# The start of a graph layer: where the first rows' numbers come from, and the order of the work up to the first pass

## The chip, the cores and the metric

The kernel runs on one core of one Trainium2 chip. The metric is the time of one execution in microseconds (us), the median of several runs. The core has five engines that each work through their own list of instructions in order and wait for each other by semaphores: TensorE (PE in the profile; its weight loads are PEld), VectorE (DVE), ScalarE (ACT), GpSimd (POOL) and SyncE (SP), which only issues transfers here. 16 DMA engines carry the transfers of SP's queue and of GpSimd's.

## The reference

A graph has 12500 nodes of 128 features and 200000 edges, sorted by destination. Each row of x is normalised and clipped at zero (h). Each edge has a score from its two nodes and a decay by its weight; of every node's incoming edges the 16 best are kept, a softmax over them weighs the messages, and the node's output is x plus a clipped sum.

```
h = max(layernorm(x), 0)
score = einsum("md,md->m", (h @ W_Q.T)[dst], (h @ W_K.T)[src]) / sqrt(128) * exp(-edge_weight)
keep the 16 best scores of each dst; alpha = softmax over the kept
agg = segment_sum(alpha * (h[src] @ W_msg.T), dst)
out = x + relu(h @ W_self.T + agg)
```

## The kernel before

**Tiling.** The edges stand in 112 groups of 14 chunks of 128 edges (G, GC). For each chunk GpSimd issues one indirect transfer (L177, called a gather here) which fetches the 128 rows that the chunk's edges name as their sources: 64 KB into hs[:, j, :]. A group's buffer hs is one of eight. 1548 gathers are issued, one after the other. The built program lets each gather wait for the landing of the eighth gather before it.

**Two kinds of gathers.** The rows of h are first written to a table in DRAM, h_tab. It is not ready at the start, so the first four groups (RAW, 56 gathers) fetch raw rows of x, which are normalised in the buffer afterwards: statistics by row_stats (L202), then one ScalarE activation for a row of 128 edges (normed, L223), or two VectorE instructions (L249, L251). From group 4 on a group is let go in pairs of gathers (let_go, L191): VectorE copies two columns of indices into a tile ix (L199), and the two gathers read it. This copy stands in VectorE's list at a chosen place, so a gather can't start before VectorE has come that far.

**Before the loop (L270 to L476).** The order is written by hand. SP loads src as rows (L290 to L294), then x in six parts (L313), then the weights, the destinations and the edge weights. GpSimd makes constants and clears alz[1] (L337). VectorE turns the sources into float (L361, L362), TensorE transposes them so that each chunk's 128 numbers stand in 128 partitions (to_columns, L296), VectorE converts them to indices (L364), and the raw gathers follow. The six parts of x are then normalised by VectorE and ScalarE in turn and written to h_tab (L373). After that come the raw statistics of groups 0 and 1 (L387), the distances of the destinations (rel, L416), the raw rows of group 0 (L418), a comparison of neighbours (L420) and a scan over it (L422), which gives every edge its place among its node's edges, the raw rows of group 1 (L424), and three sets of 14 or 15 transposes or products through PSUM: pd from rel (L432, L434), pd from the scan (L437), the decays exp(-weight) (L439). They all go through the PSUM banks "q", of which there are three. VectorE ends with checks (L441 to L470) and the last nodes' numbers, idxo (L476).

**Pools.** These tiles lie in the pools edges and prep. Both are given back at the end of this part, and the pool win of the main loop gets their space.

**The loop (L762).** Pass i, from -3 on, works on several groups at once: for group i the scores (L618), for group i+1 the distances (far_of, L571; away, L594, each a matmul into the one bank "a" and a ScalarE square), for i-1 the places of the scores, for i-2 the choice of the 16 best, for i-3 the weighted sums (L709), which are the last reader of that group's hs, for i-4 and i-5 the output. Before the first scores, group 0 needs hT (L552), q, far, to_e (L576), pdT (L585), aw and opo (L598). The raw rows of groups 2 and 3 get their statistics at the end of pass 0 (L836) and are normalised in passes 1 and 2, three times three rows on ScalarE and four on VectorE (raw_finished, L243). From pass 2 on pass i lets go of the last pairs of group i+4 and the first two of group i+5 (more, L775):

```
            g, k = (i + 4, k + 2) if k < 5 else (i + 5, k - 5)
```

So the first pair of group 8, whose hs is the buffer that held group 0, is let go in pass 3, at more(5), after the sums of group 0.

Of the kernel before, what the change touches and what calls it, by code (L numbers as in the profile page):

```python
# [76 lines left out]
def gnn_layer(  # L77
# [55 lines left out]
    def bank(tag, bufs):  # L133
        return psum.tile([P, 512], F32, tag=tag, bufs=bufs, name=tag)
# [36 lines left out]
    T = [{} for _ in range(G)]  # L171

    def gather(g, j0, j1, index, table=h_tab):
        if j0 == 0:
            T[g]["hs"] = rows_pool.tile([P, GC, D], F32, name="hs", bufs=8)
        for j in range(j0, j1):
            nc.gpsimd.indirect_dma_start(  # L177
                out=T[g]["hs"][:, j, :], out_offset=None, in_=table[0:N, :],
                in_offset=bass.IndirectOffsetOnAxis(ap=index(j), axis=0))
# [43 lines left out]
    def normed(rows, n0, n1, rs, sm):  # L223

        if n0 == 0:
            nc.vector.reciprocal(rs, rs)
            nc.vector.scalar_tensor_tensor(sm, sm, -0.5, rs, op0=OP.mult, op1=OP.mult)
        for t in range(n0, n1):
            nc.scalar.activation(rows[:, t, :], rows[:, t, :], AF.Relu, bias=sm[:, t:t + 1],
                                 scale=rs[:, t:t + 1])  # L230
# [3 lines left out]
        T[g]["raw"] = row_stats(rows_pool, T[g]["hs"], own[g], f"r{g % 2}")  # L234

    def raw_normed(g):
        normed(T[g]["hs"], 0, own[g], *T[g]["raw"])


    def raw_begun(g):  # L240
        normed(T[g]["hs"], 0, 1, *T[g]["raw"])

    def raw_finished(g, part):  # L243
        rows, (rs, sm) = T[g]["hs"], T[g]["raw"]
        if part < 3:
            normed(rows, 1 + 3 * part, 4 + 3 * part, rs, sm)
            return
        for t in range(10, own[g]):
            nc.vector.tensor_scalar(rows[:, t, :], rows[:, t, :], rs[:, t:t + 1], sm[:, t:t + 1],  # L249
                                    op0=OP.mult, op1=OP.add)  # L250
            nc.vector.tensor_scalar(rows[:, t, :], rows[:, t, :], 0.0, None, op0=OP.max)  # L251

    w0 = rows_pool.tile([P, NJ], F32, name="w0")
    zpad = rows_pool.tile([P, D], F32, name="zpad")
# [12 lines left out]
    sizes = [n for n in sizes + [left] if n]  # L267
    cuts = [(a, b) for a, b in ((0, HP - HP % 16), (HP - HP % 16, HP)) if a < b]
    by_part = lambda a: a[0:N, :].rearrange("(p t) d -> p t d", t=HT)
    with tc.tile_pool(name="edges", bufs=1) as ep, ExitStack() as stage:  # L270
        prep = stage.enter_context(tc.tile_pool(name="prep", bufs=1))
        RL = HALO + RW
        src_r = ep.tile([RR, RL], I32, name="src_r")
        h0 = src_r.bitcast(F32)
# [18 lines left out]

                nc.sync.dma_start(t[RF:RF + 1, REM:RW], a[0:RW - REM].rearrange("(p c) -> p c", p=1))  # L294

        def to_columns(rows, lo, put):  # L296

            for j0 in range(0, CPR, 4):
                j1 = min(j0 + 4, CPR)
                pt = bank("q", 3)  # L300
                for j in range(j0, j1):
                    nc.tensor.transpose(pt[:, (j - j0) * RR:(j - j0 + 1) * RR],
                                        rows[:, lo + j * P:lo + (j + 1) * P], ident[0:RR, 0:RR])
                put(lambda t: t[:, j0:j1, :],
                    pt[:, 0:(j1 - j0) * RR].rearrange("e (j p) -> e j p", p=RR))


        load_rows(src_r, src)
        xs, t = [], 0
        for i, n in enumerate(sizes):  # L310
# [23 lines left out]
                              bass.AP(dst.tensor, dst.offset + p0 * RW - HALO, [[RW, p1 - p0], [1, RL + P]]))  # L334
        nc.sync.dma_start(dst_r[k:k + 1, 0:HALO + M - k * RW], dst[k * RW - HALO:M].rearrange("(p c) -> p c", p=1))
        load_rows(ew_r, ew)
        nc.gpsimd.memset(alz[1], 0.0)  # L337
        nc.vector.memset(ones, 1.0)
        nc.vector.memset(onerow, 1.0)
        nc.vector.memset(zrow, 0.0)  # L340
# [21 lines left out]
        nc.vector.tensor_copy(src_f[:, 4 * P:], src_r[:, 4 * P:RW])  # L362
        by_chunk = lambda t: t[:, 0:RR * CPR].rearrange("e (p j) -> e j p", j=CPR)
        to_columns(src_f, 0, lambda at, p: nc.vector.tensor_copy(at(by_chunk(idx_all)), p))  # L364
        for g in range(RAW):
            gather_at_once(g, x)
        stat = {0: row_stats(prep, xs[0][2], sizes[0], "x0")}

# [4 lines left out]
                nc.sync.dma_start(by_part(h_tab)[a:b, t0:t0 + n, :], xg[a:b])  # L373

        for i in range(len(xs)):
            if i + 1 < len(xs):
                stat[i + 1] = row_stats(prep, xs[i + 1][2], sizes[i + 1], f"x{i + 1}", lambda: finish(i))
            else:
                finish(i)
# [36 lines left out]
        nc.vector.tensor_scalar(rel, dst_f[:, HALO:], dst_f[:, HALO - 1:HALO], 1.0, op0=OP.subtract, op1=OP.subtract)  # L416
        let_go(RAW, 2)
        raw_normed(0)  # L418
        nc.vector.memset(h0[:, 0:1], 0.0)
        nc.vector.tensor_tensor(h0[:, 1:RL], dst_f[:, 1:RL], dst_f[:, 0:RL - 1], op=OP.is_equal)  # L420
        let_go(RAW, 3)
        nc.vector.tensor_tensor_scan(h1, h0, h0, 0.0, op0=OP.mult, op1=OP.add)  # L422
        let_go(RAW, 4)
        raw_normed(1)  # L424
        bb = rows_pool.tile([P, 2, G], F32, name="bb")
        nc.vector.tensor_copy(bb, pb[:, 0:2 * G].rearrange("p (a g) -> p a g", a=2))

        for j0 in range(0, NJ, 4):
            j1 = min(j0 + 4, NJ)
            pt = bank("q", 3)  # L430
            for j in range(j0, j1):
# [2 lines left out]
            nc.vector.tensor_tensor(pd[:, 16 + j0:16 + j1, :],  # L434
                                    pt[:, 0:(j1 - j0) * RR].rearrange("e (j g) -> e j g", g=RR),
                                    bc(w0[:, j0:j1], RR), op=OP.subtract)
        to_columns(h1, HALO, lambda at, p: nc.scalar.copy(at(pd), p))  # L437
        nc.scalar.copy(pd[:, GC:NJ, 0:G - 1], pd[:, 0:1, 1:G])
        to_columns(ew_r, 0, lambda at, p: nc.scalar.activation(at(by_chunk(dec_all)), p, AF.Exp, scale=-1.0))  # L439
        let_go(RAW, 5)  # L440
        nc.vector.scalar_tensor_tensor(h0[:, HALO:RL], dst_f[:, HALO - 1:RL - 1], 0.0, dst_f[:, HALO:RL],  # L441
                                       op0=OP.add, op1=OP.is_gt, accum_out=bad[0:RR, 1:2])
# [78 lines left out]
    with tc.tile_pool(name="win", bufs=2) as win:  # L521
# [40 lines left out]
        def far_of(g, b):  # L562
            n0, n1 = 4 * P * b, min(4 * P * (b + 1), chunks[g] * P)
            if n0 >= n1:
                return
            if b == 0:
                T[g]["far"] = win.tile([P, NJ * P], BF16, name="far")
            pr = bank("a", 1)
            nc.tensor.matmul(pr[:, 0:n1 - n0], lhsT=upper(ident[0:RR, g:g + 1]).to_broadcast([RR, P]),  # L569
                             rhs=rel[:, n0:n1], start=True, stop=True)  # L570
            nc.scalar.activation(T[g]["far"][:, n0:n1], pr[:, 0:n1 - n0], AF.Square, bias=minus)  # L571
# [15 lines left out]
        def away(g, b):  # L587
            if b == 0:
                T[g]["aw"] = win.tile([P, 2 * NJ * KM], BF16, name="aw")
            n0, n1 = 400 * b, 400 * b + 400  # L590
            pr = bank("a", 1)
            nc.tensor.matmul(pr[:, 0:400], lhsT=T[g]["pdT"],  # L592
                             rhs=minus_at.rearrange("k w j s -> k (w j s)")[:, n0:n1], start=True, stop=True)
            nc.scalar.activation(T[g]["aw"][:, n0:n1], pr[:, 0:400], AF.Square)  # L594
# [167 lines left out]
        for i in range(-3, G - 1):  # L762
            at(i + 3, load_nodes)
            for g in slowly:
                if g - PASSES - 1 <= i < g - 1:
                    some_rows(g, i - g + PASSES + 1)
            if i == 8:
                nc.sync.dma_start(h_tab[N:N + P, :], zpad)
                nc.sync.dma_start(x_end[XT:XT + P, :], zpad)
                nc.sync.dma_start(x_end[0:XT, :], x[N - XT:N, :])  # L770
            def raw(part):
                if i in (1, 2):
                    raw_finished(i + 1, part)

            def more(k):  # L775

                if i in (-1, 0, 1):
                    g = i + 6
                else:
                    g, k = (i + 4, k + 2) if k < 5 else (i + 5, k - 5)  # L780
                    if g < 8:
                        return
                if i >= -1 and g < G:
                    let_go(g, k)

            at(i, q_to_edges, 0)
            at(i - 5, output)
            at(i - 5, store)
            at(i - 3, weights)
            more(0)  # L790
            at(i - 4, sums_turned)
            at(i + 1, far_of, 0)
            at(i - 4, sums_turned_out)
            at(i + 1, q_out)
            at(i, q_to_edges, 1)
            at(i + 1, far_of, 1)
            raw(0)
            for b in range(3):
                at(i - 1, slots_by_node, b)
            at(i + 1, far_of, 2)  # L800
            more(1)
            at(i - 2, best)
            more(2)
            at(i - 2, sum_of_exps)
            at(i - 1, slots_out)
            raw(1)
            at(i, q_to_edges, 2)
            at(i + 1, far_of, 3)
            raw(2)
            at(i + 2, h_turned)  # L810
            at(i, scores, 0)
            more(3)
            at(i + 1, to_edges)
            at(i + 2, h_turned_out)
            at(i - 2, kept_to_edges)
            at(i - 1, node_by_slots)
            at(i + 1, edges_turned)
            at(i - 3, sums, 0)
            at(i, scores, 1)
            more(4)  # L820
            at(i + 1, away, 0)
            at(i, q_to_edges, 3)
            at(i - 2, one_over_sum)
            at(i + 1, away, 1)
            at(i - 3, sums, 1)
            at(i, scores, 2)
            at(i - 2, on_edges)
            more(5)
            at(i + 1, away, 2)
            at(i - 3, sums_out)  # L830
            at(i - 4, products)
            at(i - 2, exps)
            at(i + 1, places)
            at(i, scores, 3)
            at(i, scores_in_slots)
            if i == 0:  # L836
                raw_stats(2)
                raw_stats(3)
                raw_begun(2)
                raw_begun(3)  # L840
            if i in (1, 2):
                raw_finished(i + 1, 3)
            more(6)
            at(i + 2, q_made)
            if i > 0 and later:
                later.pop(0)()
# [267 lines left out]
```

## Time and profile before

| | us |
|---|---|
| median of 5 runs (2002.68 to 2006.04) | 2003.6 |
| the profiled execution | 2007.59 |
| its span | 2005.8 |
| GpSimd busy | 1490.0 (74%) |
| TensorE busy | 1564.2 (78%) |
| VectorE busy | 1275.1 (64%) |
| ScalarE busy | 1023.0 (51%) |
| first gather, start | 10.22 |
| last gather, start | 1971.56 |

The profile comes from one execution. A line of groups gives line, engine, operation, output<-inputs and count, then the busy time and the mean in ns, then the idle time before these instructions and what ended it. A line of a timeline gives start, duration, engine, line, operation, tiles, shapes and count, and in brackets the idle time of the engine before it and who ended it; "issue" there means that nothing in the profile shows what ended it. A line of stretches gives from:to, the length, the busy time of TensorE, its weight loads, VectorE, ScalarE and GpSimd with the number of instructions, then the granted clock of TensorE, the busy share of the DMA engines and GB/s.

### The profile page before, as it was taken

What the parts mean: (1) busy time and instruction counts of PE and PEld (TensorE: products, weight loads), DVE (VectorE), ACT (ScalarE), POOL (GpSimd) and SP (SyncE); (2) the same over time, 40 slices, a digit from 0 to 9 for tenths busy, and PEclk for the clock granted to TensorE, in tenths of its full rate; (3) what the DMA queues carried; (4) which work ended last, traced back from release to release, by engine and by line L of the source; (5) the groups of instructions that cost most, each with busy time, mean ns of one, the idle gap of its engine ahead of it and who ended that gap; (6) DMA issues with size and microseconds to landing.
All of it is one profiled execution on the core that took longest, in us unless ns stands there. A gap on an engine that the chain in (4) does not pass through costs nothing. (4 is left out here: it accounts for less than half of the span.)

```text
span 2005.8 us, 48358 instructions
## 1 busy us (share of the span) xinstructions
PE 1564.2 (78%) x13800; PEld 1291.7 (64%) x13801; DVE 1275.1 (64%) x7022; ACT 1023.0 (51%) x2190; POOL 1490.0 (74%) x1565
## 2 busy tenths in 40 slices
PE   0369999877787778887878887887778777877886
PEld 0247877766666666666666666666666666666665
DVE  7567787666666566666656666666666666666655
ACT  6766666554445454544544444554544444544441
POOL 6777777777777777777777777777777777777773
PEclk9979999998989898999989989999989999898888
DMA  9522322222222222222222222222222222222221
GB/s 239 164 61 61 81 67 66 66 67 68 68 66 66 66 66 63 65 67 66 67 65 66 66 63 65 66 66 67 66 67 66 67 65 64 66 66 65 65 57 29
DMA packets 104911, 143.89 MB, mean 72 GB/s; under 512 B 32758, under 2 KB 77957, under 8 KB 103870
## 3 DMA queue, kind: packets, MB, share of 16 engines
q0 software_dynamic: 49664, 101.75, 20.1%
q1 hardware_dynamic: 54972, 38.99, 7.1%
q8 instruction: 109, 1.79, 0.4%
q14 instruction: 166, 1.36, 0.2%
HBM read 126.80 MB, written 14.40 MB: 70 GB/s over the span
## 5 line engine op out<-in xcount | busy, mean ns | idle before, releaser
L177 POOL DMA_INDIRECT hs<-h_tab,ix x1492 | 1421.0, 952 | 458.0 <-issue 302.2
L618 DVE SCALAR_TENSOR_TENSOR prod<-hs,dec_all,q 128x128 f32<-128x128 f32 x1659 | 505.0, 344 | 296.1 <-DMA hs<-h_tab,ix 258.5
L571 ACT ACTIVATE far<-a,minus 128x512 bf16<-128x512 f32 (+1 forms) x447 | 294.4, 659 | 508.7 <-PE a L569 498.9
L609 PE MATMUL q<-q,to_e 128*128 128x128 f32 x3348 | 509.4, 299 | 0.0
L609 PEld LDWEIGHTS q<-q,to_e 128*128 128x128 f32 x3348 | 479.5, 212 | 33.7 <-DVE prod L618 11.9
L709 PE MATMUL e<-hs,alz 128*128 128x128 f32 x3210 | 418.1, 282 | 0.0
L709 PEld LDWEIGHTS e<-hs,alz 128*128 128x128 f32 x3210 | 375.8, 191 | 26.9 <-issue 19.2
L594 ACT ACTIVATE aw<-a 128x400 bf16<-128x400 f32 x336 | 169.1, 503 | 314.1 <-PE a L592 308.5
L648 DVE TENSOR_SCALAR ell<-slots,e 128x40 f32<-128x40 f32 x112 | 28.2, 252 | 350.4 <-PE e L634 271.3
L717 PE MATMUL s<-ident,agn 128*128 128x128 f32 x112 | 38.4, 342 | 260.7 <-DVE kept L698 257.7
L576 ACT ACTIVATE to_e<-far 128x1920 f32<-128x1920 bf16 x112 | 201.5, 1799 | 3.5
L569 PE MATMUL a<-rel,ident 112*128 112x512 bf16 (+1 forms) x447 | 192.9, 432 | 8.1 <-ACT far L571 8.1
L717 PEld LDWEIGHTS s<-ident,agn 128*128 128x128 f32 x112 | 17.0, 152 | 276.0 <-issue 270.6
L634 PE MATMUL e<-opo,sl 128*41 128x40 f32 x3348 | 186.0, 228 | 0.0
L634 PEld LDWEIGHTS e<-opo,sl 128*41 128x41 f32 x3348 | 172.3, 142 | 11.7
L618 DVE DVE_READ_ACCUMULATOR prod<-hs,dec_all,q 128x1 f32 x1659 | 137.4, 83 | 0.2
L598 ACT ACTIVATE opo<-aw 128x1200 f32<-128x1200 bf16 x112 | 134.1, 1197 | 0.1
L199 DVE COPY ix<-idx_all 128x2 int32<-128x2 int32 x754 | 133.7, 193 | 0.0
L592 PE MATMUL a<-minus_at,pdT 32*128 32x400 bf16 x336 | 115.3, 343 | 19.5 <-ACT pdT L585 9.6
L677 PEld LDWEIGHTS <-to_e 128*128 128x128 bf16 x1674 | 49.9, 97 | 98.2 <-DVE km L660 96.1
L677 PE MATMUL x<-km,to_e 128*128 128x43 bf16 x1674 | 61.1, 183 | 66.6 <-DVE km L660 66.0
L626 DVE TENSOR_TENSOR sl<-opo,s 128x600 f32<-128x600 f32 x112 | 87.7, 783 | 4.0
(188 smaller groups left out, 1680.3 us busy)
## 6 DMA issues: line engine op xcount, KB each, us to landing
late<-h_tab SPq DMA_DIRECT2D x1920, 0.5 KB
hs<-h_tab,ix POOLq DMA_INDIRECT x1492
h_r<-h_tab SPq DMA_DIRECT2D x112, 64.0 KB
x_t<-in_x_dram SPq DMA_DIRECT2D x108, 64.0 KB
out_dram<-o SPq DMA_DIRECT2D x108, 64.0 KB
xg<-in_x_dram SPq DMA_DIRECT2D x2, 1400.0 KB
h_tab<-xg SPq DMA_DIRECT2D x2, 1400.0 KB
xg<-in_x_dram SPq DMA_DIRECT2D x1, 1120.0 KB
```

The lines of the kernel that those rows point to most:

```text
L177: nc.gpsimd.indirect_dma_start(out=T[g]["hs"][:, j, :], out_offset=None, in_=table[0:N, :], in_offset=bass.IndirectOffsetOnAxis(ap=index(j ...
L199: nc.vector.tensor_copy(ix[:, j0:j1], idx_all[:, GC * g + j0:GC * g + j1])
L569: nc.tensor.matmul(pr[:, 0:n1 - n0], lhsT=upper(ident[0:RR, g:g + 1]).to_broadcast([RR, P]), rhs=rel[:, n0:n1], start=True, stop=True)
L571: nc.scalar.activation(T[g]["far"][:, n0:n1], pr[:, 0:n1 - n0], AF.Square, bias=minus)
L576: nc.scalar.activation(T[g]["to_e"][:, 0:n], T[g]["far"][:, 0:n], AF.Relu, bias=1.0, scale=-1.0)
L592: nc.tensor.matmul(pr[:, 0:400], lhsT=T[g]["pdT"], rhs=minus_at.rearrange("k w j s -> k (w j s)")[:, n0:n1], start=True, stop=True)
L594: nc.scalar.activation(T[g]["aw"][:, n0:n1], pr[:, 0:400], AF.Square)
L598: nc.scalar.activation(T[g]["opo"].rearrange("e w j s -> e (w j s)"), T[g]["aw"], AF.Relu, bias=1.0, scale=-1.0)
L609: nc.tensor.matmul(pq[:, (j - j0) * P:(j - j0 + 1) * P], lhsT=T[g]["to_e"][:, j * P:(j + 1) * P], rhs=T[g]["q"], start=True, stop=True)
L618: nc.vector.scalar_tensor_tensor(prod, rows_of(g, j), dec_all[:, c:c + 1], T[g]["pq", b][:, (j % 4) * P:(j % 4 + 1) * P], op0=OP.mult, op1 ...
L634: nc.tensor.matmul(et[0:KM + 1, STEP * j:STEP * j + WN], lhsT=sl1[g % 2][:, j, :], rhs=T[g]["ow"][:, j, :], start=False, stop=(j == n - 1))
L709: nc.tensor.matmul(T[g]["pa"], lhsT=alz[g % 2][:, WW * j + PRE:WW * j + PRE + P], rhs=rows_of(g, j), start=(j == 0), stop=(j == n - 1))
```

## The change

- The sources of the first four chunks are loaded once more, by a transfer of 512 single numbers straight into 128 partitions (idx_0); it is the first load on SP's queue. The first four gathers read it. The other ten of group 0 are issued after the indices' conversion, as before, and then groups 1 to 3.
- alz[1] is cleared by VectorE, ahead of the statistics of the sixth part of x, and no longer by GpSimd.
- Of group 0's 14 raw rows, nine are normalised by ScalarE and five by VectorE (after pd is taken from rel). Of group 1's rows only the first is done before the loop; the other 13 follow in pass 0, as groups 2 and 3 have it in passes 1 and 2, and pass 0's four VectorE rows come ahead of the statistics of groups 2 and 3.
- The decays' transposes and exponentials come before the matmuls of L432, and they and the scan's transposes go through the banks "a", "e" and "x" in turn.
- The comparison and the scan are done in four quarters, each scan starting from the last value of the quarter before.
- Group 0's far and aw use the three banks "q" in place of "a".
- The pool prep is opened before edges instead of after it; both still end together.

```diff
     def gather(g, j0, j1, index, table=h_tab):
-        if j0 == 0:
+        if "hs" not in T[g]:
...
     def raw_normed(g):
-        normed(T[g]["hs"], 0, own[g], *T[g]["raw"])
...
+        normed(T[g]["hs"], 0, 9, *T[g]["raw"])
+
+    def raw_on_dve(g, n0):
         rows, (rs, sm) = T[g]["hs"], T[g]["raw"]
...
+        for t in range(n0, own[g]):
             nc.vector.tensor_scalar(rows[:, t, :], rows[:, t, :], rs[:, t:t + 1], sm[:, t:t + 1],
                                     op0=OP.mult, op1=OP.add)
             nc.vector.tensor_scalar(rows[:, t, :], rows[:, t, :], 0.0, None, op0=OP.max)
...
-    with tc.tile_pool(name="edges", bufs=1) as ep, ExitStack() as stage:
-        prep = stage.enter_context(tc.tile_pool(name="prep", bufs=1))
+    with tc.tile_pool(name="prep", bufs=1) as prep, tc.tile_pool(name="edges", bufs=1) as ep:
...
-                pt = bank("q", 3)
+                pt = bank(*banks[j0 // 4 % len(banks)])
...
+        EARLY = 4
+        idx_0 = ep.tile([P, EARLY], I32, name="idx_0")
+        nc.sync.dma_start(idx_0, src[0:EARLY * P].rearrange("(j p) -> p j", p=P))
         load_rows(src_r, src)
...
-        nc.gpsimd.memset(alz[1], 0.0)
+        gather(0, 0, EARLY, lambda j: idx_0[:, j:j + 1], x)
...
-        for g in range(RAW):
+        gather(0, EARLY, own[0], lambda j: idx_all[:, j:j + 1], x)
+        for g in range(1, RAW):
             gather_at_once(g, x)
...
+            if i + 2 == len(xs):
+                nc.vector.memset(alz[1], 0.0)
...
         raw_normed(0)
+        others = (("a", 1), ("e", 1), ("x", 1))
+        to_columns(ew_r, 0, lambda at, p: nc.scalar.activation(at(by_chunk(dec_all)), p, AF.Exp, scale=-1.0),
+                   others)
         nc.vector.memset(h0[:, 0:1], 0.0)
-        nc.vector.tensor_tensor(h0[:, 1:RL], dst_f[:, 1:RL], dst_f[:, 0:RL - 1], op=OP.is_equal)
+        quarters = [(a, min(a + RL // 4, RL)) for a in range(0, RL, RL // 4)]
+        for a, b in quarters:
+            nc.vector.tensor_tensor(h0[:, max(a, 1):b], dst_f[:, max(a, 1):b], dst_f[:, max(a, 1) - 1:b - 1],
+                                    op=OP.is_equal)
         let_go(RAW, 3)
-        nc.vector.tensor_tensor_scan(h1, h0, h0, 0.0, op0=OP.mult, op1=OP.add)
+        for a, b in quarters:
+            nc.vector.tensor_tensor_scan(h1[:, a:b], h0[:, a:b], h0[:, a:b],
+                                         0.0 if a == 0 else h1[:, a - 1:a], op0=OP.mult, op1=OP.add)
         let_go(RAW, 4)
-        raw_normed(1)
+        raw_begun(1)
...
-        to_columns(h1, HALO, lambda at, p: nc.scalar.copy(at(pd), p))
+        raw_on_dve(0, 9)
+        to_columns(h1, HALO, lambda at, p: nc.scalar.copy(at(pd), p), others)
         nc.scalar.copy(pd[:, GC:NJ, 0:G - 1], pd[:, 0:1, 1:G])
-        to_columns(ew_r, 0, lambda at, p: nc.scalar.activation(at(by_chunk(dec_all)), p, AF.Exp, scale=-1.0))
...
-            pr = bank("a", 1)
+            pr = bank("q", 3) if g == 0 else bank("a", 1)
...
-                if i in (1, 2):
+                if i in (0, 1, 2):
                     raw_finished(i + 1, part)
...
+            if i in (0, 1, 2):
+                raw_finished(i + 1, 3)
             if i == 0:
                 raw_stats(2)
                 raw_stats(3)
                 raw_begun(2)
                 raw_begun(3)
-            if i in (1, 2):
-                raw_finished(i + 1, 3)
```

The line `pr = bank(...)` is changed in this way in far_of and in away.

More of the change, by code (lines that the diff above doesn't have):

```diff
@@ L236, in raw_normed @@
     def raw_normed(g):
-        normed(T[g]["hs"], 0, own[g], *T[g]["raw"])
+        normed(T[g]["hs"], 0, 9, *T[g]["raw"])
+    def raw_on_dve(g, n0):
+        rows, (rs, sm) = T[g]["hs"], T[g]["raw"]
+        for t in range(n0, own[g]):
+            nc.vector.tensor_scalar(rows[:, t, :], rows[:, t, :], rs[:, t:t + 1], sm[:, t:t + 1],
+                                    op0=OP.mult, op1=OP.add)
+            nc.vector.tensor_scalar(rows[:, t, :], rows[:, t, :], 0.0, None, op0=OP.max)
     def raw_begun(g):
@@ L243, in raw_finished @@
     def raw_finished(g, part):
-        rows, (rs, sm) = T[g]["hs"], T[g]["raw"]
         if part < 3:
[L246 to L251, printed above, removed]
+            normed(T[g]["hs"], 1 + 3 * part, 4 + 3 * part, *T[g]["raw"])
+        else:
+            raw_on_dve(g, 10)
     w0 = rows_pool.tile([P, NJ], F32, name="w0")
@@ L294, in load_rows, with to_columns @@
                 nc.sync.dma_start(t[RF:RF + 1, REM:RW], a[0:RW - REM].rearrange("(p c) -> p c", p=1))
-        def to_columns(rows, lo, put):
+        def to_columns(rows, lo, put, banks=(("q", 3),)):
             for j0 in range(0, CPR, 4):
                 j1 = min(j0 + 4, CPR)
-                pt = bank("q", 3)
+                pt = bank(*banks[j0 // 4 % len(banks)])
                 for j in range(j0, j1):
@@ L590, in away @@
             n0, n1 = 400 * b, 400 * b + 400
-            pr = bank("a", 1)
+            pr = bank("q", 3) if g == 0 else bank("a", 1)
             nc.tensor.matmul(pr[:, 0:400], lhsT=T[g]["pdT"],
```

## The prediction

> **What bounds the kernel now.** I read the table of instruction groups first, then GpSimd's timeline at the start, the middle and the end, then VectorE's and ScalarE's timelines up to 170 us, and last the table by stretches. The chain of the last work is of no use: it covers only the last 5 us. The group of gathers:
>
> ```profile
> L177 POOL DMA_INDIRECT hs<-h_tab,ix x1492 | 1421.0, 952 | 458.0 <-issue 302.2
> ```
>
> 1492 gathers and the 56 raw ones before them. In GpSimd's timeline one starts 1.248 us after the other (0.944 busy, 0.304 gap), so 1548 of them need 1932 us of a 2005.8 us span. The timeline shows where that row of gathers breaks:
>
> ```profile
> 162.33 0.94 POOL L177 DMA_INDIRECT hs<-h_tab,ix  x1 [0.30 <-DVE prod L618]
> 163.58 0.94 POOL L177 DMA_INDIRECT hs<-h_tab,ix  x1 [0.30 <-issue]
> 166.33 1.20 POOL L177 DMA_INDIRECT hs<-h_tab,ix  x1 [1.80 <-PE a L592]
> 169.39 0.95 POOL L177 DMA_INDIRECT hs<-h_tab,ix  x1 [1.87 <-issue]
> 170.65 0.95 POOL L177 DMA_INDIRECT hs<-h_tab,ix  x1 [0.30 <-issue]
> ...
> 1971.56 0.94 POOL L177 DMA_INDIRECT hs<-h_tab,ix  x1 [0.30 <-DVE prod L618]
> ```
>
> The row at 166.33 is gather 112 (counted from 0), the first of group 8. There are eight buffers hs, so it writes the one that group 0 leaves free. It waits for two things: the copy of its indices on VectorE (L199, done at 165.10) and the last matmul of group 0's sums (L709, about 165.6). From 169.39 to 1971.56 nothing holds GpSimd up but short stretches of some 0.3 us, and the end follows 34 us after the last gather. So **the end is the start of gather 113 plus a constant**, and the change counts only by what it does to that start. Gather 112 would have been ready at 164.8 (163.58 + 1.25): GpSimd was 1.5 us early for it. The limit before 166 us is the computing chain of the first four groups, and GpSimd's own start at 10.22 is not.
>
> **The change, part by part.**
>
> *GpSimd's start: worth nothing.* The clearing of alz[1] (2.28 us from 4.08) leaves GpSimd, and four gathers need only the new 512-number load. They can start at about 4.4; the load is issued at 0.77 and lands some 2 us after its issue, as h_r does (73.12 to 74.9). Gather 4 needs the second conversion of L364, done at 10.4, plus 0.5 as the first gather took after its own, plus the later src_r below: 11.7 instead of 15.41. GpSimd is 3.7 us ahead and waits 3.7 us longer at gather 112. The cleared tile goes to VectorE, into the 4.05 us in which that engine waits for a square root:
>
> ```profile
> 39.52 0.67 DVE L208 BATCH_NORM_STATS2 stx<-xg 125x6 f32<-125x128 f32 x3
> ...
> 44.25 0.32 DVE L226 RECIPROCAL rsx<-rsx 125x25 f32<-125x25 f32 x1 [4.05 <-ACT rsx L220]
> ...
> 71.45 4.02 DVE L422 TENSOR_TENSOR_SCAN h<-src_r 112x1856 f32<-112x1856 f32 x1
> ...
> 83.74 0.17 DVE L476 CAST idxo<-t 128x4 int32<-128x4 f32 x1
> ```
>
> The same clearing of alz[0] took 2.06 there: hidden, and +2.1 if the cover went.
>
> *The new load and the earlier gathers: +1.9.* The load stands ahead of four loads of src and twelve of x on SP's queue. Its price is not in the trace. At least 0.22 (one row, L292); at most 3.3 (b_i's 111 single numbers took 0.89 to issue: 0.006 us each, times 512, plus 0.22). The loads of 128 partitions (0.33 to 0.43, so 0.001 us a row) are nearer to its 128 partitions: I take 0.8. Behind it the transfers never rest:
>
> ```profile
> 10.00:66.00 56.00, 2.02 (x9) 1.30 (x7) 39.19 (x213) 40.98 (x111) 37.01 (x39) 1.00 1.01 267
> ...
> 82.00:164.00 82.00, 55.17 (x333) 40.86 (x334) 44.07 (x250) 52.74 (x100) 62.19 (x66) 0.79 0.24 62
> ```
>
> (A share of 1.01 of the DMA engines at 267 GB/s in the first line.) Some 4.5 gathers more get in among the loads of x, 64 KB each, 0.25 us each: 1.1. That is on the path: the fourth and fifth parts of x land at 24.66 and 33.1, VectorE waits for each (2.13 and 2.07 us), and from 34.38 to 61.06 ScalarE normalises without a rest. Bounds 0.4 to 4.6.
> The Trainium skill, "DMA: Bandwidth & Descriptors", Specifications, speaks against the new load: it asks for at least 512 B per transfer, and here each is 4 B. It gives no price per number; on its side is b_i's row, and the sum with 3.3 would be 2.5 more.
>
> *VectorE up to the copy of idxo: +0.3 on the path.* The built program shows that the first tile of the window's pool (hT of group 0, L552) waits for all that the pools edges and prep still do, in both kernels: the last is VectorE's idxo (83.74 + 0.17). Swapping the two pools does not alter that. Before, it was done while ScalarE had other work:
>
> ```profile
> 75.92 5.50 ACT L229 ACTIVATE hs<-hs,smr,rsr 128x128 f32<-128x128 f32 x14 [0.98 <-DVE smr L227]
> ...
> 81.32 1.61 ACT L437 CAST pd<-q 128x448 bf16<-128x448 f32 x4
> ...
> 87.07 0.30 ACT L552 COPY hT<-s 128x128 f32<-128x128 f32 x1
> ...
> 88.68 0.69 ACT L571 ACTIVATE far<-a,minus 128x512 bf16<-128x512 f32 x1 [1.31 <-PE a L569]
> ...
> 90.04 0.69 ACT L571 ACTIVATE far<-a,minus 128x512 bf16<-128x512 f32 x1 [0.52 <-PE a L569]
> ...
> 95.12 0.25 ACT L585 CAST pdT<-a 32x128 bf16<-32x128 f32 x1
> ...
> 98.66 1.20 ACT L598 ACTIVATE opo<-aw 128x1200 f32<-128x1200 bf16 x1
> ```
>
> Afterwards ScalarE would be ready for hT at about 81.6: it has 18 rows less to normalise (0.39 each), and the exponentials and their table (1.28 + 2.84) lie beside VectorE's comparison and scan. But VectorE now gets there later: five raw rows of group 0 (ten instructions; four rows took 2.51 from 132.93 to 135.44, so 0.63 each) are 3.1, and the scan in quarters costs 0.3 (each needs the last one's end; bounds 0 and 0.6; the comparison's quarters overlap like independent instructions, 0). 83.9 + 3.4 = 87.3, hT at 87.4. What ScalarE gains, 5.5 us, is lost in this wait; behind hT stand all of group 0's distances.
> The skill's "SBUF — State Buffer", Who interferes with whom, says that a VectorE instruction with two SBUF inputs and a GpSimd instruction that reads SBUF shut each other out, by order of issue. The trace agrees: beside the scan one gather took 3.69 us. By it the quarters give GpSimd some 2 us back; they would only lengthen its wait at gather 112.
>
> *Three banks for group 0: -3.65.* Four squares go at ScalarE's own pace of 0.59 instead of 1.3; pdT comes 2.05 earlier after hT. Of the three steps behind pdT the matmuls need no release: TensorE is through after 1.3 instead of 2.9 (95.12 to 98.02), 1.6.
>
> *Group 1's raw rows in the first pass: +2.4 and +2.4.* Nine activations (3 x 1.25) now stand between the squares of group 1. They fill some 1.3 us in which ScalarE waited for TensorE (0.45 + 0.46 + 0.41), 2.4 remain up to pdT of group 1 and with it the last scores. Then four rows on VectorE (2.4, as above) ahead of the statistics of groups 2 and 3 (8.0 us), which the next pass waits for (sqrt at 118.01, squares at 119.15). Passes 1 to 3 are as before.
>
> Sum at the statistics' end, 118.62 before: +0.3 - 3.65 + 2.4 + 2.45 = +1.5, and +1.9 of transfers: **+3.4 us**. Gather 113 goes from 169.4 to 172.8, though GpSimd is free 3.7 earlier. The profiled execution took 2007.6 (span 2005.8 and 1.8 around it), the median is 4.0 below; the shift is the same for both: 2003.6 + 3.4 = **2007.0**, and 2011.0 for a profiled one.
>
> **Rivals.**
>
> *The new load is cheap, or ScalarE's chain does not feel the gathers.* Then the transfers cost 0.4: +1.9, 2005.5. For it: 13-row loads are issued in 0.39. Against: the DMA share of 1.01. Chance 0.20.
>
> *The single numbers cost what b_i's do.* 4.6 instead of 1.9: 2009.7. For it: the only row of 4-byte numbers. Chance 0.22.
>
> *The wait at gather 112 is lifted: faster.* If VectorE's idxo came by 81.5 (the raw rows found their place elsewhere) and the transfers cost under 1, the chain would be some 4.5 shorter, GpSimd's start would decide, and with it the 3.1 us lost at gathers 112 and 113 would go: at most 3.1 + 3.7 = 6.8, 1996.8; it decides from a chain more than 4.4 us shorter on. Against: VectorE's sum above leaves no such room. For: 5.5 us of free ScalarE, and a granted clock of 0.79 between 82 and 164 that can change with TensorE's gaps by some 2 us either way. Chance 0.13.
>
> **How the numbers follow.** My forecast, 2005.8 to 2008.5, has 0.45. The range reaches up to the dear load with 2 us of clock on top, and down past the cheap load less 2 us of clock, part of the way to the third rival, so that no more than 2 in 10 is left out: 2001 to 2011. A measurement of this kernel tells about 0.2%, 4 us, from no change. Slower by more: 0.40 (the dear case and nearly half of the forecast); within: 0.48; faster: 0.12.
>
> **What would show it.** Right: gather 0 near 4.4, gather 4 near 11.7; hT of group 0 ended by VectorE's idxo at 87 to 90; an idle stretch of 7 to 10 us at gather 112, and gather 113 near 172.8; last x part 1 to 3 us later. Wrong: hT at 82 to 84, or gather 113 before 168, or a second long wait of GpSimd at a later group.

## The result, and the profile after

The changed kernel takes 2008.4 us (median; 2005.5 to 2011.2), the one before 2004.0 (median of 45 runs, 1999.1 to 2008.6). The ratio is 1.0021, with an interval of 1.0016 to 1.0027: slower by 4.2 us (3.2 to 5.4). The forecast was 2007.0. The profiled execution after took 2008.5 (span 2006.7), close to its median; that of before took 2007.6, which is 3.6 above its own. So the two profiles differ by 0.9 us only, and the 4.2 has to be read from marks inside them, not from their ends.

Two of the changed kernel's 24 executions (2040.0 and 4512.4 us) and eight of the twelve experiment runs below (3103 to 3111 us, like the kernel before beside them) were slow: the range above leaves the two out, and from the eight only the order of instructions is read.

GpSimd's group of gathers after:

```profile
L177 POOL DMA_INDIRECT hs<-h_tab,ix x1492 | 1420.2, 952 | 469.7 <-issue 305.5 <-DVE prod L634 54.6 <-DMA hs<-h_tab,ix 30.2
```

The same gathers, 11.7 us more idle time (458.0 before). GpSimd's timeline tells where it lies:

```profile
8.24 1.31 POOL L177 DMA_INDIRECT hs<-in_x_dram,idx  x1 [0.30 <-issue]
11.79 0.94 POOL L177 DMA_INDIRECT hs<-in_x_dram,idx_all  x1 [2.23 <-DVE idx_all L369]
...
154.61 0.95 POOL L177 DMA_INDIRECT hs<-h_tab,ix  x1 [0.30 <-issue]
169.09 1.19 POOL L177 DMA_INDIRECT hs<-h_tab,ix  x1 [13.53 <-PE a L608]
172.15 0.95 POOL L177 DMA_INDIRECT hs<-h_tab,ix  x1 [1.87 <-issue]
173.41 0.94 POOL L177 DMA_INDIRECT hs<-h_tab,ix  x1 [0.30 <-issue]
...
1972.80 0.94 POOL L177 DMA_INDIRECT hs<-h_tab,ix  x1 [0.30 <-DVE prod L634]
```

Gather 4 starts at 11.79 (15.41 before), gather 111 at 154.61 (163.58). Then GpSimd stands for 13.53 us at gather 112 (1.80 before) and loses all of the 9 us and 2.8 more: gather 113 at 172.15 instead of 169.39. TensorE's timeline there, first before and then after, with the copy of gather 112's indices on VectorE after:

```profile
163.74 2.05 PE L709 MATMUL e<-hs,alz 128*128 128x128 f32 x16
165.72 0.34 PE L592 MATMUL a<-minus_at,pdT 32*128 32x400 bf16 x1
```

```profile
166.50 2.05 PE L725 MATMUL e<-hs,alz 128*128 128x128 f32 x16
168.48 0.34 PE L608 MATMUL a<-minus_at,pdT 32*128 32x400 bf16 x1
```

```profile
167.69 0.16 DVE L199 COPY ix<-idx_all 128x2 int32<-128x2 int32 x1
```

The first row of each pair is the second half of group 0's sums, the last reader of the buffer. "PE a L608" in GpSimd's row names only the matmul that stands behind it in TensorE's list; in the program's order gather 112 comes ahead of that one and waits for the sums, done at 168.55. The other thing that it waits for, the copy, was done at 167.85, only 0.70 us sooner, and also 0.70 sooner before (165.09 and 165.79). Both belong to pass 3, so both are of the computing chain.

The two stretches that were shown of before (us, busy time of PE, PEld, DVE, ACT and POOL, granted clock as a share of TensorE's full clock, DMA share, GB/s):

```profile
10.00:66.00 56.00, 2.91 (x13) 2.09 (x11) 40.52 (x207) 40.30 (x107) 37.14 (x40) 1.00 1.01 271
82.00:164.00 82.00, 47.62 (x303) 35.62 (x302) 47.60 (x262) 49.46 (x99) 56.19 (x58) 0.69 0.22 58
```

The transfers are as full as before (1.01). Between 82 and 164 TensorE gets through 303 matmuls instead of 333, at a granted clock of 0.69 instead of 0.79. VectorE's timeline after:

```profile
25.93 0.68 DVE L208 BATCH_NORM_STATS2 stx<-xg 125x6 f32<-125x128 f32 x3 [2.26 <-DMA xg<-in_x_dram]
...
34.73 0.68 DVE L208 BATCH_NORM_STATS2 stx<-xg 125x6 f32<-125x128 f32 x3 [2.46 <-DMA xg<-in_x_dram]
...
41.55 2.06 DVE L383 MEMSET alz<- 128x2400 f32 x1 [0.44 <-issue]
...
45.76 0.32 DVE L226 RECIPROCAL rsx<-rsx 125x25 f32<-125x25 f32 x1 [1.61 <-ACT rsx L220]
...
73.26 1.12 DVE L437 TENSOR_TENSOR_SCAN h<-src_r 112x464 f32<-112x464 f32 x1
74.42 3.62 DVE L437 TENSOR_TENSOR_SCAN h<-src_r,h 112x464 f32<-112x464 f32 x3
...
89.02 0.17 DVE L492 CAST idxo<-t 128x4 int32<-128x4 f32 x1
```

The fourth and fifth parts of x come 1.18 and 1.57 us later than before (24.75 and 33.16 there). The clearing of alz[1] lies in the wait for the square root, of which 1.61 is left. The scan in quarters ends 4.78 us after its start (4.02 before), and idxo ends at 89.19 instead of 83.91. ScalarE's timeline after:

```profile
71.09 3.57 ACT L229 ACTIVATE hs<-hs,smr,rsr 128x128 f32<-128x128 f32 x9 [3.60 <-DVE smr L227]
...
82.77 0.30 ACT L455 COPY pd<-pd 128x111 bf16<-128x111 bf16 x1
89.34 0.27 ACT L568 COPY hT<-s 128x128 f32<-128x128 f32 x1 [6.27 <-issue]
90.92 0.69 ACT L587 ACTIVATE far<-q,minus 128x512 bf16<-128x512 f32 x1 [1.31 <-PE q L585]
...
91.65 1.75 ACT L587 ACTIVATE far<-q,minus 128x512 bf16<-128x512 f32 x3
...
95.28 0.25 ACT L601 CAST pdT<-a 32x128 bf16<-32x128 f32 x1
...
97.46 1.20 ACT L614 ACTIVATE opo<-aw 128x1200 f32<-128x1200 bf16 x1
...
121.91 0.21 ACT L220 ACTIVATE rsr<-rsr 128x14 f32<-128x14 f32 x1 [3.43 <-DVE rsr L219]
```

ScalarE is free at 83.07 and stands 6.27 us before hT, which follows idxo's end by 0.15. The squares of group 0 run without a gap behind the first, and opo comes 1.2 sooner than before (98.66). The second square root of the statistics of groups 2 and 3 stands at 121.91, before at 118.01: what the banks won is more than gone by the end of the first pass.

### The profile page after: what moved, and what is told of

Same layout as the page of the kernel before. It is cut to its first block, busy times and chain, and to the rows that moved or that the text cites. A ratio compares the mean times of both kernels' runs of the same rounds, so it can differ in the third digit from the quotient of the medians.

```text
span 2006.7 us, 48379 instructions
## 1 busy us (share of the span) xinstructions
PE 1563.3 (78%) x13800; PEld 1292.6 (64%) x13801; DVE 1279.6 (64%) x7047; ACT 1018.8 (51%) x2181; POOL 1483.5 (74%) x1564
## 5 line engine op out<-in xcount | busy, mean ns | idle before, releaser
L608 PE MATMUL a<-minus_at,pdT 32*128 32x400 bf16 x333 | 114.0, 342 | 17.4 <-ACT pdT L601 8.8
```

What stands on the lines that cost most here:

```text
L608: nc.tensor.matmul(pr[:, 0:400], lhsT=T[g]["pdT"], rhs=minus_at.rearrange("k w j s -> k (w j s)")[:, n0:n1], start=True, stop=True)
```

## The experiments

**My theory** is the prediction's: up to gather 112 the computing chain (the x part, VectorE up to idxo, hT, group 0's distances, the first pass) decides, since gather 112 writes the buffer that group 0's sums still read; GpSimd's earlier start is worth nothing, and the change lengthens that chain. **The rivals:** GpSimd's own start or its stalls further on decide; or the end is set by TensorE and the later groups, whatever happens at gather 112.

Times are given as ratios to the kernel before on the same chip, with their intervals.

**Nine buffers in the changed kernel (a_nine, a_nine_again).** The wait at gather 112 is taken away by taking away what it waits for: there is another buffer, so that group 8 does not use group 0's. Room for it comes from ew_r, which uses alz[1] until that is needed; group 8 and the later ones are let go one pass earlier. So the edit takes away both things that gather 112 waits for: the sums, and the late copy of its indices. A ninth buffer with the copies left in their place was not run; by the changed kernel's rows gather 112 could then not have started ahead of 167.85.

```diff
-            T[g]["hs"] = rows_pool.tile([P, GC, D], F32, name="hs", bufs=8)
+            T[g]["hs"] = rows_pool.tile([P, GC, D], F32, name="hs", bufs=9)
...
-        ew_r = ep.tile([RR, RW], F32, name="ew_r")
+        ew_r = alz[1][0:RR, 0:RW]
...
-            if i + 2 == len(xs):
-                nc.vector.memset(alz[1], 0.0)
...
         nc.vector.tensor_copy(idxo, t1)
+        nc.vector.memset(alz[1], 0.0)
...
-                    g, k = (i + 4, k + 2) if k < 5 else (i + 5, k - 5)
+                    g, k = (i + 5, k + 2) if k < 5 else (i + 6, k - 5)
```

> The changed kernel with nine buffers hs instead of eight; each group is let go one pass earlier accordingly. The room comes from ew_r, which uses alz[1]; alz[1] is cleared on VectorE behind idxo instead of between the x parts. Theory (gather 112 waits for group 0's sums only because its buffer is used again): gather 112 follows at once, at 155.9, gather 113 at 157.1; gather 126 is now the first that uses a buffer again, its sums are done at 168.6 and GpSimd comes there at 173.3: no wait. Time 2008.4 - 15.0 = 1993.4, up to 1997 with more stalls beside the first passes. Rival one (the end is set by something else, the computing chain of later groups or TensorE): 2004 to 2008. Rival two (the wait appears again in full at gather 126): gather 127 near 185 to 190, time 2004 or more.

This run took 3110.7 us, the kernel before 3110.1. The second:

> The same kernel as a_nine, since on the chip of that call the kernel before took 3110 us (granted clock 0.74, engines short of instructions from 55 us on), so that GpSimd was not the limit and the run could not tell the theories apart. Where the kernel before takes about 2004 us: Theory: gather 112 follows at once near 155.9 and gather 113 at 157.1, gather 126 does not wait, time 15.0 below the changed kernel's 2008.4, 1993.4, up to 1997 with more stalls. Rival one (the end is set by the computing chain or TensorE): 2004 to 2008. Rival two (the wait comes back at gather 126): 2004 or more. Where the kernel before takes 3110 us again: no difference, 3105 to 3115.

1993.1 us, ratio 0.9948 (0.9935 to 0.9961): 0.3 us from the theory's number, and 15 us under the changed kernel. GpSimd's timeline of a_nine_again at the same gathers, 111 to 113:

```profile
153.38 0.94 POOL L177 DMA_INDIRECT hs<-h_tab,ix  x1 [0.30 <-issue]
154.63 1.28 POOL L177 DMA_INDIRECT hs<-h_tab,ix  x1 [0.30 <-DVE prod L633]
156.22 0.95 POOL L177 DMA_INDIRECT hs<-h_tab,ix  x1 [0.30 <-issue]
```

No wait at gather 112, and none at gather 126, where a buffer is used again for the first time. Group 0's sums are nearly where they were (their second half begins at 167.32, in the changed kernel at 166.50); only nobody waits for them. Both rivals of the theory fall: the end goes with gather 113, which is 15.9 us sooner than in the changed kernel, while the ratio is 0.0073 lower (1.0021 to 0.9948), 14.6 us.

**Nine buffers in the kernel before (b_nine).** The same edit; alz[1] is still cleared on GpSimd at the start, ahead of ew_r's load, and once more behind idxo.

> The kernel before with nine buffers hs and the same rearrangement as in a_nine (ew_r in alz[1]; VectorE clears it behind idxo); GpSimd's start stays as it was. Theory (with the wait at gather 112 gone GpSimd's own start decides): gather 112 at 164.9, gather 113 at 166.1 instead of 169.4, time 2004.0 - 3.3 = 2000.7, 1998 to 2001; the changed kernel with nine buffers (1993.1) is then 5 to 8 us faster than it, which is what the early start is worth once nothing waits for the computing chain. Rival (the nine buffers help for another reason, the same 15 us for either kernel): 1989. Rival (the early start is worth nothing even so): 1993.

2001.0 us, ratio 0.9979 (0.9970 to 0.9988). GpSimd's timeline of b_nine, gathers 111 to 113:

```profile
160.02 0.94 POOL L177 DMA_INDIRECT hs<-h_tab,ix  x1 [0.30 <-issue]
161.27 0.95 POOL L177 DMA_INDIRECT hs<-h_tab,ix  x1 [0.30 <-DVE prod L619]
162.53 0.95 POOL L177 DMA_INDIRECT hs<-h_tab,ix  x1 [0.30 <-issue]
```

This turns the sign of the change round. With eight buffers it costs 0.0021 of the time; with nine it saves 0.0031 (0.9979 to 0.9948; 0.0015 to 0.0047 with the two intervals taken together), 6.2 us, and gather 113 is 6.3 us sooner (156.22 against 162.53). GpSimd's lead, from the earlier start and from the quarters of the scan together, is worth something as soon as nothing waits for the computing chain.

**The earlier start alone (b_early).** The kernel before with idx_0, four gathers from it, and alz[1] cleared between the parts of x.

```diff
+        EARLY = 4
+        idx_0 = ep.tile([P, EARLY], I32, name="idx_0")
+        nc.sync.dma_start(idx_0, src[0:EARLY * P].rearrange("(j p) -> p j", p=P))
         load_rows(src_r, src)
...
-        nc.gpsimd.memset(alz[1], 0.0)
+        gather(0, 0, EARLY, lambda j: idx_0[:, j:j + 1], x)
...
-        for g in range(RAW):
+        gather(0, EARLY, own[0], lambda j: idx_all[:, j:j + 1], x)
+        for g in range(1, RAW):
             gather_at_once(g, x)
...
+            if i + 2 == len(xs):
+                nc.vector.memset(alz[1], 0.0)
```

> The kernel before with one part of the change: idx_0, the four early gathers from it, and alz[1] cleared on VectorE between the x parts. Theory (eight buffers: gather 112 waits for the computing chain; GpSimd's start is worth nothing, the transfers cost 1.55): first gather at 4.3 instead of 10.2, the fourth and fifth parts of x 1.2 to 1.5 us later, GpSimd 8 to 9 us sooner at gather 112 and waiting 11 to 13 us there instead of 1.8, gather 113 at 170.9 instead of 169.4, time 2004.0 + 1.55 = 2005.6, 1.0008 of the kernel before. Rival one (GpSimd's start counts): gather 113 at 160 to 164, time 1995 to 1998, 0.997 or less. Rival two (the transfers cost nothing): 1.0000. Where the kernel before takes 3100 us: no difference.

2002.5 us beside 2001.1, ratio 1.0008 (0.9999 to 1.0017): the theory's number; a gain of 6 us is excluded, a cost of nothing is not. VectorE's timeline of b_early has the fourth and fifth parts of x 0.86 and 0.83 us later than before:

```profile
25.61 0.68 DVE L208 BATCH_NORM_STATS2 stx<-xg 125x6 f32<-125x128 f32 x3 [2.01 <-DMA xg<-in_x_dram]
...
33.99 0.68 DVE L208 BATCH_NORM_STATS2 stx<-xg 125x6 f32<-125x128 f32 x3 [2.03 <-DMA xg<-in_x_dram]
```

ScalarE's last part of x moves by 0.84 (55.19 to 56.03), hT by 0.98, pdT by 0.98, the statistics' end by 1.00: nearly one delay that runs through the whole chain. And GpSimd, which starts 5.9 us sooner, waits for it:

```profile
159.10 0.94 POOL L177 DMA_INDIRECT hs<-h_tab,ix  x1 [0.30 <-issue]
165.43 1.19 POOL L177 DMA_INDIRECT hs<-h_tab,ix  x1 [5.38 <-PE a L598]
168.49 0.95 POOL L177 DMA_INDIRECT hs<-h_tab,ix  x1 [1.88 <-issue]
```

Its head start at gather 111 is only 4.5 us, not the 8 to 9 that I expected: most of the other 4.5 of the changed kernel comes from the comparison and the scan in quarters (last section). In this one profile gather 113 is even 0.9 us sooner than in that of before, because passes 1 to 3 took 1.9 us less with the same instructions; the times do not show it.

**Group 1's raw rows ahead of the loop (a_raw1_ahead, a_raw1_again).** The changed kernel with that one part undone: all 14 rows on ScalarE where it waits for hT anyway.

```diff
-        raw_begun(1)
+        normed(T[1]["hs"], 0, own[1], *T[1]["raw"])
         bb = rows_pool.tile([P, 2, G], F32, name="bb")
...
-                if i in (0, 1, 2):
+                if i in (1, 2):
                     raw_finished(i + 1, part)
...
-            if i in (0, 1, 2):
+            if i in (1, 2):
                 raw_finished(i + 1, 3)
```

> The same kernel as a_raw1_ahead (group 1's 14 raw rows on ScalarE ahead of the loop), where the kernel before takes about 2004 us. Theory (with eight buffers gather 112 waits for the computing chain): hT stays at 89.3 to 89.9, the first pass loses 3.9 to 4.8 us, gather 112 at 164.3 to 165.5, gather 113 at 167.4 to 168.6, time 2003.6 to 2004.5. Rival one (stalls behind gather 113): 2008.4. Rival two (the nine activations lie in idle time of ScalarE): 2006 and above. Where the kernel before takes 3110 us: no difference.

(The first run of it, a_raw1_ahead, took 3105.6 us beside 3110.1.) 2004.5 us beside 2005.8, ratio 0.9993 (0.9984 to 1.0002); against the changed kernel's 1.0021 that is 0.0028, 5.6 us. ScalarE's timeline of a_raw1_again:

```profile
85.27 0.30 ACT L455 COPY pd<-pd 128x111 bf16<-128x111 bf16 x1
89.30 0.27 ACT L568 COPY hT<-s 128x128 f32<-128x128 f32 x1 [3.74 <-issue]
...
117.23 0.21 ACT L220 ACTIVATE rsr<-rsr 128x14 f32<-128x14 f32 x1 [3.22 <-DVE rsr L219]
```

hT has not moved, though ScalarE did five microseconds more work ahead of it; the statistics' end is 4.68 us sooner. GpSimd's timeline of the same kernel:

```profile
153.58 0.94 POOL L177 DMA_INDIRECT hs<-h_tab,ix  x1 [0.30 <-issue]
163.90 1.19 POOL L177 DMA_INDIRECT hs<-h_tab,ix  x1 [9.37 <-PE a L608]
166.96 0.95 POOL L177 DMA_INDIRECT hs<-h_tab,ix  x1 [1.87 <-issue]
```

Gather 113 is 5.2 us sooner than in the changed kernel. Rival two of this run falls: nearly nothing of the nine activations had been hidden.

**Group 0's last raw rows behind idxo (a_rows_late, a_rows_late_again).** VectorE's ten instructions are moved:

```diff
-        raw_on_dve(0, 9)
         to_columns(h1, HALO, lambda at, p: nc.scalar.copy(at(pd), p), others)
...
         nc.vector.tensor_copy(idxo, t1)
+        raw_on_dve(0, 9)
```

> The same kernel as a_rows_late (VectorE's ten instructions for group 0's last raw rows behind idxo), where the kernel before takes about 2004 us. Theory: idxo and with it hT come 2.7 us sooner, hT at 86.6; all behind it 2.7 sooner, gather 113 at 169.4 instead of 172.1, time 2005.7. Rival one (hT waits for something else than idxo): hT at 89.3, time 2008.4. Rival two (group 0's first scores now wait for the rows): scores as in the changed kernel, time 2008.4. Where the kernel before takes 3110 us: no difference.

The two runs took 3107.9 us beside 3110.1 and 3103.3 beside 3104.5, so the time of 2005.7 was not put to the test. The order could be read. VectorE's timeline of a_rows_late_again:

```profile
114.40 0.17 DVE L491 CAST idxo<-t 128x4 int32<-128x4 f32 x1
114.47 0.34 DVE L242 TENSOR_SCALAR hs<-hs,rsr,smr 128x128 f32<-128x128 f32 x1
...
117.27 0.23 DVE L244 TENSOR_SCALAR hs<-hs 128x128 f32<-128x128 f32 x1
```

and ScalarE's:

```profile
112.99 0.29 ACT L454 COPY pd<-pd 128x111 bf16<-128x111 bf16 x1
114.72 0.27 ACT L568 COPY hT<-s 128x128 f32<-128x128 f32 x1 [1.44 <-issue]
```

hT stands 0.15 us behind idxo's end (114.57), as in the changed kernel, a_raw1_again and a_nine_again (0.15 or 0.16), and it does not wait for the rows, which go on to 117.5. Rival one is out: it is idxo that hT waits for, where ScalarE is free by then. In the kernel before hT comes 3.16 us after idxo, when ScalarE is free. The first run, a_rows_late, fits less well: there hT came 2.26 us behind idxo and 0.93 behind ScalarE's last instruction, though still ahead of the last row; what held it is not shown.

**Four further runs, at 3104 to 3110 us.** The changed kernel with GpSimd's start as before (3110.4 us beside 3110.1); the question it was to settle was settled by b_early:

> The changed kernel with GpSimd's start as before: no idx_0 and no early gathers, alz[1] cleared on GpSimd. Theory (GpSimd's start is worth nothing, the transfers cost 1.55): first gather near 10.2, GpSimd arrives at gather 112 6 to 9 us later and waits 3 to 6 us there instead of 13.5; x parts 1.2 to 1.5 us sooner, gather 113 at 170.6, time 2006.8. Rival (GpSimd's start counts one to one): time 2014. Rival (the transfers cost nothing): 2008.4.

The kernel before with group 0's distances in the banks q, by the two lines of the diff that say so (3108.3 beside 3104.5). The part alone is so left without a time:

> The kernel before with one part of the change: group 0's distances in the three banks q. Theory: four squares without waiting (2.05 us) and the three steps behind pdT (1.6 us) make the chain 3.65 us shorter, group 0's sums end near 162.1 and the copy of the indices near 161.5, before GpSimd comes to gather 112 at 164.8: no wait there, gather 113 at 166.1 instead of 169.4, and the 1.87 us behind gather 112 are gone too: time 2004.0 - 3.3 = 2000.7, and not lower, since GpSimd's start is now the limit, as with nine buffers (2001.0). Rival one (the banks' gain is given back in passes 0 to 3): gather 113 between 167 and 169.4, 2002 to 2004. Rival two (the 1.87 us behind gather 112 stay): 2002.5.

Nine buffers with both shortenings of the chain, a_raw1_ahead's and a_rows_late's, twice (3104.1 beside 3107.6, and 3106.8 beside 3110.0). Whether the chain no longer counts at all with nine buffers was therefore not measured:

> The changed kernel with nine buffers hs (as a_nine), and with two shortenings of the computing chain: group 1's raw rows on ScalarE ahead of the loop (which alone took gather 113 from 172.1 to 167.0 with eight buffers), and VectorE's ten instructions for group 0's last raw rows behind idxo. Theory (hT waits for idxo; with nine buffers GpSimd's start decides and the chain no longer): hT at 86.6 instead of 89.6, group 0's sums end some 7.5 us sooner than in a_nine, and the time stays within 1 us of a_nine: 0.9948 of the kernel before, 1993. Rival one (the chain still counts): 4 to 7 us less, 1986 to 1989. Rival two (hT waits for something else than idxo): hT at 89.3 to 89.6. Where the kernel before takes 3100 us or more: no difference, and only hT's place could be read.

> The same kernel as a_nine_chain (nine buffers; group 1's raw rows on ScalarE ahead of the loop; VectorE's ten instructions for group 0's last raw rows behind idxo). Theory (hT waits for idxo; with nine buffers GpSimd's start decides and the chain no longer): idxo ends near 86.4 and hT stands at 86.6 instead of 89.6, group 0's sums end some 7.5 us sooner than in the changed kernel's 168.55, and the time stays that of a_nine: 0.9948 of the kernel before, 0.993 to 0.996. Rival one (the chain still counts): 4 to 7 us less than a_nine, 0.991 to 0.993. Rival two (hT waits for something else than idxo): hT at 89.3 to 89.6. Where the kernel before takes 3100 us: no difference.

## Why the prediction held, step by step

These marks are start times in us, from the timelines of the engines named:

| mark | before | b_early | after | a_raw1_again | a_nine_again |
|---|---|---|---|---|---|
| hT of group 0 (ScalarE) | 87.07 | 88.04 | 89.34 | 89.30 | 89.62 |
| first scores' matmul (TensorE) | 98.61 | 99.59 | 97.28 | 97.25 | 97.56 |
| last statistics' square root (ScalarE) | 118.01 | 119.01 | 121.91 | 117.23 | 122.27 |
| second half of group 0's sums (TensorE) | 163.74 | 162.84 | 166.50 | 161.31 | 167.32 |
| gather 113 (GpSimd) | 169.39 | 168.49 | 172.15 | 166.96 | 156.22 |
| from gather 113 to the span's end | 1836.4 | 1831.1 | 1834.6 | 1835.9 | 1832.5 |

- *The gate.* Right: in all four profiles with eight buffers gather 113 starts 5.65 us after the second half of group 0's sums begins; with nine buffers and the earlier letting go it does not depend on them. The copy of the indices keeps as fixed a distance (4.30 us from its end to gather 113), so the constant alone does not tell the two apart; the order of their ends does.
- *GpSimd's start, worth nothing.* Right with eight buffers (b_early). Gathers 0 and 4 at 4.31 and 11.79, predicted 4.4 and 11.7; for gather 4 by luck in part, since the second conversion ended at 10.70, not 10.4, and the first gather followed its own by 0.29, not 0.5, two slips that cancel. The wait at gather 112 was 13.5 instead of 7 to 10, a miss: GpSimd was 9.0 us ahead at gather 111, not 3.7, and of the difference the quarters gave some 3 us (last section). For the same reason the prediction's 6.8 us for a wait that is lifted was too small: with nine buffers the changed kernel is 0.0052, 10.4 us, under the kernel before.
- *The transfers, +1.9.* Measured 1.55 at ScalarE's last part of x in the changed kernel (55.19 to 56.74) and 0.84 at the same place in b_early, 1.0 from hT on. Both kernels have the same early load and early gathers, so why they differ stays open. idx_0 took 0.46 us to issue, not 0.8, and the first load of x is issued 0.59 later (2.90 against 2.31); how the delay is shared between this and the gathers is not shown. The Trainium skill ("DMA: Bandwidth & Descriptors", Specifications) gives 512 B as the least size of a transfer for full rate. Here 512 numbers of 4 B landed 2.2 us after their issue began (0.78 to 3.0) and the whole early start cost 1.0, so the price by b_i's row, and the rival that rested on it, were too dear. (That rival's sum was also 0.2 too high: 3.3 and 1.1 are 4.4, not 4.6, so 2009.5.)
- *VectorE up to idxo, +0.3.* Measured +0.7: 89.34 less 87.07 is 2.27, less 1.55. The five rows took 2.68 (3.1 predicted), but the quarters of comparison and scan together some 1.0 (0.3 predicted). The mechanism, hT behind idxo, is shown by the four kernels named above.
- *Three banks, -3.65.* hT to the first scores: 11.54 before, 7.94 after, so -3.60. As one part alone it has no time.
- *Group 1's rows in the first pass, +2.4 and +2.45.* First scores to the last statistics' square root: 19.40 before, 24.63 after, +5.23; with the rows undone 19.98. Up to pdT of group 1 it is +2.28 (8.38 and 10.66), so the first term was right. From there it is +2.95 (11.02 and 13.97): the three steps behind pdT wait longer for TensorE (0.60, 1.52 and 0.57 us against 0.43, 1.12 and 0.57), which the prediction left out.
- *Sum at the statistics' end, +3.4.* Measured +3.90 at the last statistics' square root. At gather 113 it was +2.76, as passes 1 to 3 took 1.1 us less than before. The four profiles with eight buffers have 43.8 to 45.7 us for that stretch, with the same instructions in it; TensorE's granted clock differs between them (0.65, 0.70 and 0.61 from 124 to 140 us in before, b_early and after), but not in one order with the time, so the cause stays open.
- *The end is gather 113 plus a constant.* Only nearly: the last line of the table varies by 5 us. Some 3 of these lie behind the last gather (31.2 us in a_nine_again, 34.2 in before), where the granted clock stayed at 1.00 up to 1977 us in the one and fell to 0.88 (1970 to 1977 us) and 0.72 (1984 to 1990) in parts of the other; the rest are mostly single gathers held up by 0.3 to 0.6 us. So the 2011.0 that was predicted for a profiled execution was 2.5 too high, and two single profiles can differ by 0.9 us where the medians differ by 4.2. The +3.9 at the statistics' end lies in the medians' interval (3.2 to 5.4), the +2.76 at gather 113 does not; with one profile of each kernel that is no proof.

The forecast was 1.4 us short, 0.4 of it because the kernel before now has a median of 2004.0 instead of 2003.6. By terms: 0.35 too much for the transfers, 0.4 too little for VectorE, 0.4 too little for the first pass, so part of the closeness is errors that cancel. The largest single loss, and one that a_raw1_again avoids, is the place of group 1's rows: undone, the changed kernel can't be told from the one before (0.9993, 0.9984 to 1.0002).

## What to carry to other kernels

Before an engine's early start is counted as a gain, look for the first wait of that engine that another chain ends: here 9 us of lead turned into 9 us more of waiting. If the wait is for a buffer used again, one more buffer, with its transfers let go earlier to match, may be worth more than a shortening of the chain (0.73% in the changed kernel, where the best shortening measured gave 0.28%, but only 0.21% in the kernel before), and it can turn the sign of the other edits. Work belongs into the idle time of the engine that waits, not into the pass that others wait for: the rest of group 1's rows left hT where it was when they stood ahead of it, and cost 4.7 us behind it.

## What the runs showed of the hardware

**VectorE's scan and GpSimd's gathers.** The gather beside the whole scan in b_early, and that beside the quarters in the changed kernel, each in GpSimd's timeline:

```profile
73.52 3.69 POOL L177 DMA_INDIRECT hs<-in_x_dram,idx_all  x1 [0.30 <-issue]
```

```profile
73.29 1.85 POOL L177 DMA_INDIRECT hs<-in_x_dram,idx_all  x1 [0.30 <-issue]
```

All the gathers beside comparison, scan and the check behind them lost 7.2 us in b_early and 3.5 in the changed kernel (6.3 in before, 3.5 in a_raw1_again and 2.7 in a_nine_again). It fits the rule of the Trainium skill ("SBUF — State Buffer", Who interferes with whom) that a VectorE instruction with two inputs in SBUF and a GpSimd instruction that reads SBUF lock each other out, one instruction at a time. For what the quarters give GpSimd the prediction took 2 us; it was 2.9 against the kernel before and 3.8 against b_early.

**Behind the wait at gather 112 GpSimd loses a second time.** In the four profiles with eight buffers gather 113 came 1.87 or 1.88 us after gather 112's end, whether the wait ahead of that had been 1.80 or 13.53 us; the usual gap is 0.30, and with nine buffers it was 0.30 here too. A wait alone does not bring it: behind the 2.23 us ahead of gather 4 the next gap was 0.30. What gather 113 waits for is not shown.
